# A gated cross-attention layer: the order of TensorE's work between attention groups, planned with a count of PSUM banks and copy times

## The chip, the cores and the metric

The kernel runs on one core of a Trainium2 chip. The metric is the device time of one execution in microseconds (us). Three runs of the kernel before took 2751.24, 2752.05 and 2752.25 us; the median is 2752.05 us. The profile is of one further execution, recorded by the hardware profiler.

## The reference, cut to what matters

Four batches of 256 rows of width 512 attend to a context of 1601 rows each, with 32 query heads in 8 key/value heads (4 query heads share one). Then a feed-forward part with a router follows. All is in float32.

```
x   (4, 256, 512)   ctx (4, 1601, 512)
q   = layernorm(x) @ Wq + bq                 # 8 heads x 4 groups x 128
k,v = split(ctx @ Wkv + bkv)                 # 8 heads x 128 each
a   = softmax(q k^T / sqrt(128))             # over the 1601 context rows
x   = x + tanh(g_xattn) * (a v @ Wo + bo)
x   = x + tanh(g_ffn) * ffn(layernorm(x))    # base product, router (2 of 8), low-rank parts
```

## The kernel before, in words

**Groups.** A head here is a key/value head with its four query heads. The 256 rows of a batch are cut in two (`l` is 0 or 1), so there are 4 x 8 x 2 = 64 groups, each with 128 rows times 4 query heads, which is 512 columns. In `run_group` (L866) TensorE alternates between score products of the current group (`score_unit`, matmul at L641) and value products of the group before it (`av_unit`, L691): 13 context tiles each, the last one with 65 rows. ScalarE copies each score tile out of PSUM (L648), VectorE keeps a running maximum (L593), then reduces it over partitions (`spread`, L595 to L615), subtracts it from the seven score tiles (L663), and ScalarE takes the exponential (L664). These steps are the softmax of the group; they go on while TensorE does something else.

**Windows.** That something else is done in the window behind each group, `window` (L890): q products for the next head (`q_steps`, four items `pq`, L354), the output product of the group before (`out_steps`, `po`, L714, added to x by VectorE at L721), and the products that make the keys and values of heads two at a time (`pair_steps`, L426). A pair's keys are made while the pair before it is being worked on; its values are made in the window behind its own first group. So the four groups of a pair have four windows, called W0 to W3 here:

- W0, even head, `l` = 0: the values of this pair, due at once
- W1, even head, `l` = 1: q of the odd head, due at once; the keys of the coming pair begin
- W2, odd head, `l` = 0: more of the keys; q of the next head begins
- W3, odd head, `l` = 1: the rest of both, due at once

At the end of a batch (heads 6 and 7) there are differences: the context and x of the next batch are transposed around the group and window of head 6, `l` = 1, and the next keys begin one window later.

**Block products.** Keys and values are made with seven block products in place of eight (a Strassen-like scheme), numbered 1 to 7 in `step` (L500). The context is halved, and each half is cut in two sub-blocks of 384 columns, so a pair has 14 product steps for keys and 14 for values, plus a `tail` for the last 65 context rows (L544). For each sub-block, products 1, 6, 5 and 3 add up in one PSUM bank called x, with a copy by ScalarE after each (L490, L494); product 2 has a bank z of its own, added by VectorE (L498); products 7 and 4 add up in a bank y, read by VectorE after 5 and after 4. So product 6 must wait for the copy after 1, and 4 for VectorE's add after 5, and so on.

**PSUM.** Five banks (`ps`, L109) serve all of this, two more hold scores, one holds the value product.

**Order.** TensorE's order is written out by hand (`manual_schedule`, L905): the order in which the Python functions are called is the order of its queue. The other engines' queues are ordered by the framework. A step is a tuple of cost, lag and function. `clock["now"]` counts planned nanoseconds: `mm_cost(512)` is 857. A `Task` holds steps in a fixed order, and is ready when its lag has passed (`ready`, L839). `window` sums one common credit over all tasks (cost divided by the windows left), takes the first ready task of the list at each step (`next_task`, L854), and afterwards `flush` (L859) does what is due. In a pair's task both sub-blocks alternate: 1 1 2 2 6 6 7 7 5 5 tail 3 3 4 4.

**Loads.** Weights of keys and values share one buffer (`load_pair`, L186), as do those of q (`load_wq`) and of the output (`load_wo`): each is loaded by SyncE's queue once the one before was used. GpSimd forms weight sums after the load (L209).

Of the kernel before, what the change touches and what calls it, by code (L numbers as in the profile page):

```python
# [15 lines left out]
P = 128  # L16
# [5 lines left out]
E = 8  # L22
# [5 lines left out]
def flamingo_kernel(  # L28
# [43 lines left out]

    nc = tc.nc
# [16 lines left out]
    NPAIR = len(pairs)  # L90
    AHEAD = 1
# [17 lines left out]
    ps = ctx.enter_context(tc.tile_pool(name="ps", bufs=5, space=bass.MemoryType.PSUM))  # L109
# [115 lines left out]
    def ffn_weight_steps():  # L225
# [21 lines left out]
        def step(o):  # L247
            def run():
                if o < NC:
                    load(o + 1)  # L250
                    dst, n = base_t[:, :, o * P : (o + 1) * P], P
                else:
                    dst, n = ra[:, :, E * R :], E
                transpose_rows(staged.pop(o), n, dst, f"base_{o}")
            return NC * TR_COST, LAG_DMA, run
# [8 lines left out]
    LAG_EVAC, LAG_COPY, LAG_O = 1500, 4000, 6000  # L264

    def x_steps(b, lag):
# [17 lines left out]
        def turn(l):  # L284
# [5 lines left out]
            return NC * TR_COST, lag, run  # L290
# [3 lines left out]
    def ctx_steps(b):  # L294
# [13 lines left out]
        def step(i):  # L308
            def run():
                if i + STAGE - 1 < KT:  # L310
                    load(i + STAGE - 1)
                turn_ctx(b, i, staged.pop(i))
            return NC * TR_COST, LAG_CTX, run
# [32 lines left out]
    def q_steps(b, h):  # L346
# [3 lines left out]
        def q_item(g):  # L350
# [13 lines left out]
            return NC * mm_cost(L), 0, run  # L364
# [12 lines left out]
    def plain_k_steps(b, h):  # L377

        def item(s, n):
# [13 lines left out]
            return NC * mm_cost(n), 0, run  # L393
# [3 lines left out]
    def plain_v_steps(b, hp):  # L397
# [3 lines left out]
        def item(i):  # L401
# [20 lines left out]
            return n * NC * mm_cost(WV), 0, run  # L422
# [3 lines left out]
    def pair_steps(kind, b, hp):  # L426
# [73 lines left out]
        def step(i, s):  # L500
# [26 lines left out]
            if is_k:  # L527
                return 2 * mm_cost(SUB), 0, run
            return SUB // P * 2 * mm_cost(HDIM), 0, run
# [177 lines left out]
    def out_steps(key):  # L707
# [20 lines left out]
        return [(G * mm_cost(D), LAG_O, project)] + (ffn_steps(b, l) if h == NKV - 1 else [])  # L728


    def ffn_steps(b, l):
# [78 lines left out]
        def final_item():  # L810
# [10 lines left out]
            (NC * TR_COST, LAG_NORM, turn_item),  # L821
            (NC * (mm_cost(E * R + E) + mm_cost(D) * (b == B - 1)), LAG_COPY, route_item),
            (TR_COST, LAG_ROUTE, mid_item),
            (mm_cost(D) * (1 if b == B - 1 else NC + 1), LAG_COPY, final_item),
# [7 lines left out]

    class Task:


        def __init__(self, steps, due=None):
            self.steps = deque(steps)
            self.due = due
            self.ready = clock["now"] + self.steps[0][1]  # L839
# [4 lines left out]
        def step(self):  # L844
            cost, _, fn = self.steps.popleft()
            fn()
            clock["now"] += cost
            if self.steps:
                self.ready = clock["now"] + self.steps[0][1]
            else:  # L850
                tasks.remove(self)
            return cost
# [37 lines left out]
    def window(now):  # L890

        credit = sum(t.cost() / (t.due - now + 1 if t.due is not None else 1) for t in tasks)
        while tasks and credit > 0:
            if (t := next_task()) is None:
                soon = min(t.ready for t in tasks)
                if soon > clock["now"] + LAG_EVAC:
                    break
                clock["now"] = soon
            elif t.steps[0][0] / 2 <= credit:
                credit -= t.step()  # L900
            else:
                break
        flush(lambda t: t.due is not None and t.due <= now)
# [148 lines left out]
```

## Time and profile before

| | |
|---|---|
| median of three runs | 2752.05 us |
| the profiled execution | 2752.54 us |
| its span, first to last instruction | 2750.8 us |
| mean granted clock of TensorE | 0.988 |
| TensorE matmul busy | 2653.8 us, 96% |
| VectorE busy | 2149.1 us, 78% |
| ScalarE busy | 1201.4 us, 44% |
| GpSimd busy | 166.4 us, 6% |
| DMA, mean rate | 38 GB/s |

In the profile PE is TensorE (PEld its weight loads), DVE is VectorE, ACT is ScalarE, POOL is GpSimd. A float32 matmul stands as two records, so a product over two chunks of 128 rows has four. A timeline line gives the start and length in us, the engine, the line in the kernel, the operation, and how many instructions were merged; what stands in square brackets is the idle time ahead of it and what ended it. A line of waits gives the total in us, the number of times and the longest. The two records overlap a little, so the time of a group is best read from its start to the start of the next one.

### The profile page before, as it was taken

The numbers are of one execution on the slowest core, as the hardware profiler recorded it, in microseconds if no ns is written. First come the engines' busy times: TensorE is split into PE (matmuls) and PEld (weight loads), VectorE is DVE, ScalarE is ACT, GpSimd is POOL, SyncE is SP. The second block draws the span as 40 slices with busy tenths as digits, with TensorE's granted clock in tenths as the row PEclk, the third lists the DMA queues.
The fourth block names the chain that finished last, engine by engine and source line by source line (L and its number), as shares of the span: only waits on it lengthen the run. The fifth ranks groups of instructions, "written<-read, shape, count | busy, mean of one in ns | idle before, by whom it ended". The sixth has DMA issues, their size and how long they took to land.

```text
span 2750.8 us, 25888 instructions
## 1 busy us (share of the span) xinstructions
PE 2653.8 (96%) x9317; PEld 1502.2 (55%) x9317; DVE 2149.1 (78%) x3309; ACT 1201.4 (44%) x1881; POOL 166.4 (6%) x141
## 2 busy tenths in 40 slices
PE   8999999999999999999999999999999999999997
PEld 6446555464654646546465464645556556464643
DVE  2877887878877778778886877887887777778877
ACT  2444443444534344445443444444444444434442
POOL 0001010100001000010010100100000010100100
PEclk9999999999999999999999999999999999999999
DMA  4101000121111001012010110100201101100100
GB/s 136 46 23 39 31 32 31 39 64 38 39 39 38 24 31 39 23 39 85 17 46 31 38 39 18 44 31 23 79 24 39 39 23 39 33 29 31 39 0 23
DMA packets 79289, 104.74 MB, mean 38 GB/s; under 512 B 4349, under 2 KB 37165, under 8 KB 79161
## 3 DMA queue, kind: packets, MB, share of 16 engines
q1 hardware_dynamic: 77720, 102.02, 11.7%
q8 instruction: 73, 1.20, 0.2%
q0 software_dynamic: 272, 0.53, 0.1%
q10 hardware_dynamic: 1168, 0.55, 0.1%
q14 instruction: 56, 0.45, 0.1%
HBM read 100.98 MB, written 2.10 MB: 37 GB/s over the span
## 4 chain that ended last, share of the span: by engine, by line
PE 81%; DVE 15%; ACT 2%; issue 1%; DMA 0%; ACTq 0%; DVEq 0%
PE sc L641 26%; PE av L691 22%; PE pq L354 7%; DVE p L663 5%; PE po L714 5%; PE pxv L466 5%; PE pxk L455 4%; PE pyv L466 2%; PE pyk L455 2%; DVE mx L593 1%; PE ptk L550 1%; PE pzv L466 1%; PE pzk L455 1%; PE py L761 1%; ACT p L664 1%
## 5 line engine op out<-in xcount | busy, mean ns | idle before, releaser
L641 PE MATMUL sc<-qT,kT 128*128 128x512 f32 (+1 forms) x1664 | 796.6, 604 | 32.1 <-ACT qT L361 19.5
L648 ACT COPY p<-sc 65x512 f32<-65x512 f32 x820 | 478.6, 585 | 757.0 <-PE sc L641 755.9
L691 PE MATMUL av<-p,v 65*128 65x512 f32 x1640 | 766.6, 593 | 1.6 <-ACT p L664 1.6
L593 DVE TENSOR_TENSOR mx<-mx,p 128x1024 f32<-128x1024 f32 x252 | 307.3, 1220 | 375.8 <-ACT p L648 374.0
L641 PEld LDWEIGHTS sc<-qT,kT 128*128 128x128 f32 (+1 forms) x1664 | 305.3, 189 | 440.2 <-issue 343.1
L691 PEld LDWEIGHTS av<-p,v 65*128 65x128 f32 x1640 | 310.1, 190 | 382.5 <-issue 379.8
L664 ACT ACTIVATE p<-p 65x512 f32<-65x512 f32 x442 | 425.6, 992 | 132.0 <-DVE p L663 123.9
L663 DVE TENSOR_TENSOR p<-p,res_mx 65x512 f32<-65x512 f32 x442 | 473.2, 1138 | 2.0
L593 DVE TENSOR_TENSOR sm<-sm,p 128x1024 f32<-128x1024 f32 x252 | 314.9, 1250 | 18.4
L714 PE MATMUL po<-wo,oT 128*128 128x512 f32 x512 | 232.0, 596 | 4.2 <-ACT oT L702 4.2
L354 PE MATMUL pq<-xnT,wq 128*128 128x256 f32 x1024 | 230.3, 379 | 0.0
L354 PEld LDWEIGHTS pq<-xnT,wq 128*128 128x128 f32 x1024 | 193.7, 190 | 41.8 <-issue 11.6
L209 POOL TENSOR_TENSOR wv<-wv 128x256 f32<-128x256 f32 x60 | 103.4, 1744 | 1612.0 <-DMA wv<-in_L_xattn_Wkv_dram 1610.8
L714 PEld LDWEIGHTS po<-wo,oT 128*128 128x128 f32 x512 | 96.7, 191 | 105.1 <-issue 93.6
L702 ACT ACTIVATE oT<-oT,biasT 128x512 f32<-128x512 f32 x64 | 46.2, 722 | 241.1 <-DVE oT L701 240.8
L588 DVE TENSOR_TENSOR mx<-p,p 128x1024 f32<-128x1024 f32 x63 | 79.0, 1254 | 92.1 <-ACT p L648 91.6
L209 POOL TENSOR_TENSOR wk<-wk 128x256 f32<-128x256 f32 x60 | 56.8, 967 | 789.0 <-DMA wk<-in_L_xattn_Wkv_dram 687.2
L490 ACT ACTIVATE kT<-pxk,biasT 128x384 f32<-128x384 f32 x120 | 68.4, 570 | 76.1 <-PE pxk L455 76.1
L455 PE MATMUL pxk<-ctxT,wk 128*128 128x384 f32 x240 | 100.0, 558 | 0.0
L494 ACT COPY v<-pxv 128x384 f32<-128x384 f32 x120 | 56.0, 472 | 85.6 <-PE pxv L466 85.3
L466 PEld LDWEIGHTS pxv<-wv,T 128*128 128x128 f32 x720 | 84.9, 192 | 7.2 <-issue 7.2
L466 PE MATMUL pxv<-wv,T 128*128 128x128 f32 x720 | 87.2, 275 | 0.0
(151 smaller groups left out, 2369.7 us busy)
## 6 DMA issues: line engine op xcount, KB each, us to landing
wq<-in_L_xattn_Wq_dram SPq DMA_DIRECT2D x32, 1024.0 KB, 5.2
wo<-in_L_xattn_Wo_dram SPq DMA_DIRECT2D x32, 1024.0 KB, 5.2
ctx<-in_ctx_dram SPq DMA_DIRECT2D x48, 256.0 KB, 2.7
wk<-in_L_xattn_Wkv_dram SPq DMA_DIRECT2D x60, 128.0 KB, 2.3
wv<-in_L_xattn_Wkv_dram SPq DMA_DIRECT2D x60, 128.0 KB, 2.3
xa<-in_x_dram SPq DMA_DIRECT2D x4, 512.0 KB
out_dram<-y SPq DMA_DIRECT2D x8, 256.0 KB, 2.0
base<-in_L_ffn_base_W_dram SPq DMA_DIRECT2D x4, 256.0 KB, 9.0
```

The costliest lines, as they stand in the source:

```text
L209: nc.gpsimd.tensor_tensor(w[:, out_], w[:, x_], w[:, y_], op)
L354: nc.tensor.matmul(pq[:, :L], w_t["q", b, h][:, c, g * HDIM : (g + 1) * HDIM], xnT_t[b][:, c, :], start=(c == 0), stop=(c == NC - 1),)
L455: nc.tensor.matmul(bk[:, :SUB], a(SLOT[i], c), operand(i, c, s, SUB), start=first and c == 0, stop=c == 1, skip_group_check=True,)
L466: nc.tensor.matmul(bk[:, t * HDIM : (t + 1) * HDIM], operand(i, c, s + t * P, P), a(SLOT[i], c), start=first and t == 0 and c == 0, stop=c ...
L588: nc.vector.tensor_tensor(acc, p[first], p[first + 1], op)
L593: nc.vector.tensor_tensor(acc, acc, p[j], op)
L641: nc.tensor.matmul(sc[:r, :], kT_t[b, h][:, i * P : i * P + r], qT_t[b, h][:, :, l * P : (l + 1) * P], start=True, stop=True,)
L648: nc.scalar.copy(p[:r, k, :], sc[:r, :])
L663: nc.vector.tensor_tensor(p, p, mb[:r].unsqueeze(1).to_broadcast([r, n, W]), ALU.subtract)
L664: nc.scalar.activation(p, p, AF.Exp, scale=scale)
L691: nc.tensor.matmul(av, v_t[b, h // 2][:r, i, h % 2, :], p_t[key][j][:r, k, :], start=(j == 0 and k == 0), stop=(j == NPAIR - 1 and k == le ...
L714: nc.tensor.matmul(po, oT_t[key][:, g, :], w_t["o", b, h][:, g, :], start=(g == 0), stop=(g == G - 1),)
```

## The change: what it does

Each step of a window now also says what it does with PSUM. `NBANK` is 5, and a list `free` holds the planned time at which each bank comes free. A step with a lag as its fourth member takes a bank for that long (2000 ns for ScalarE, 3000 for VectorE); product steps 1 and 7 take a bank without a term (`TAKE`), and 3 and 4 give it back. A task is ready when its lag has passed and a bank is free. Products 6, 5, 3 and 4 have lags of their own, for the copies that they follow.

The sub-blocks of a pair are no longer alternated in a fixed order. For values, each sub-block and the tail are tasks of their own, three in all, marked `chain`. For keys they are one task, one sub-block after the other, with the tail last. Within a sub-block the order is 1 2 6 7 5 3 4.

`window` gives each task a credit of its own: its cost over the windows left, or unlimited where it is due or has no due window. At each step it picks the task that can run first, a chain before others, then by place in the list. If the window's last step is not of a chain and a chain is ready, one more chain step is taken at the end.

Last, q of an odd head begins in W0 instead of W1 (except for the first head and across batches).

```diff
+    NBANK = 5
+    LAG_ACT, LAG_DVE = 2000, 3000
+    TAKE = -1
...
-            return NC * mm_cost(L), 0, run
+            return NC * mm_cost(L), 0, run, LAG_ACT
...
+            cost = 2 * mm_cost(SUB) if is_k else SUB // P * 2 * mm_cost(HDIM)
+            lag = {6: LAG_ACT - cost, 5: LAG_ACT - cost, 3: LAG_ACT, 4: LAG_DVE}.get(i, 0)
+            bank_use = {1: TAKE, 7: TAKE, 2: LAG_DVE, 3: (LAG_ACT,), 4: (LAG_DVE,)}.get(i)
+            return cost, lag, run, bank_use
...
-        subs = range(0, HK, SUB)
-        steps = [(0, 0, begin)]
-        for i in (1, 2, 6, 7, 5):
-            steps += [step(i, s) for s in subs]
-        if n:
-            steps.append((2 * NC * mm_cost(P), 0, tail))
-        for i in (3, 4):
-            steps += [step(i, s) for s in subs]
-        return steps
+        begin()
+        parts = [[step(i, s) for i in (1, 2, 6, 7, 5, 3, 4)] for s in range(0, HK, SUB)]
+        if n:
+            parts.append([(2 * NC * mm_cost(P), 0, tail, LAG_ACT)])
+        return parts
...
+    free = [0.0] * NBANK
     class Task:
+        @property
+        def ready(self):
+            use = self.use(self.steps[0])
+            if use is None or isinstance(use, tuple):
+                return self.since
+            return max(self.since, min(free, default=math.inf))
         def step(self):
+            step = self.steps.popleft()
+            step[2]()
+            clock["now"] += step[0]
+            self.credit -= step[0]
+            use = self.use(step)
+            if isinstance(use, tuple):
+                free.append(clock["now"] + use[0])
+            elif use is not None:
+                free.remove(min(free))
+                if use != TAKE:
+                    free.append(clock["now"] + use)
...
     def window(now):
-        credit = sum(t.cost() / (t.due - now + 1 if t.due is not None else 1) for t in tasks)
-        while tasks and credit > 0:
-            if (t := next_task()) is None:
-                soon = min(t.ready for t in tasks)
-                if soon > clock["now"] + LAG_EVAC:
-                    break
-                clock["now"] = soon
-            elif t.steps[0][0] / 2 <= credit:
-                credit -= t.step()
-            else:
-                break
-        flush(lambda t: t.due is not None and t.due <= now)
+        for t in tasks:
+            later = t.due - now if t.due is not None else 0
+            t.credit = t.cost() / (later + 1) if later > 0 else math.inf
+        step = None
+        while True:
+            can = [t for t in tasks if t.credit > 0 and t.steps[0][0] / 2 <= t.credit]
+            must = any(t.due is not None and t.due <= now for t in can)
+            if not can:
+                break
+            t = min(can, key=lambda t: (max(t.ready, clock["now"]), not t.chain, tasks.index(t)))
+            if t.ready > clock["now"] + LAG_EVAC and not must:
+                break
+            clock["now"] = max(clock["now"], t.ready)
+            t.step()
+            step = t
+        for t in tasks:
+            if step is not None and not step.chain and t.chain and t.ready <= clock["now"]:
+                t.step()
+                break
...
-                tasks.append(Task(pair_steps("v", *pair), now))
-            if nxt is not None and l == (0 if h % 2 == 1 and nxt[1] > 0 else NL - 1):
+                tasks.extend(Task(part, now, True) for part in pair_steps("v", *pair))
+            if nxt is not None and l == (0 if nxt[1] > 0 and hi > 0 else NL - 1):
                 tasks.append(Task(q_steps(*nxt), hi * NL + NL - 1))
...
-                tasks.append(Task(pair_steps("k", *coming), (hi | 1) * NL + NL - 1))
+                steps = sum(pair_steps("k", *coming), [])
+                tasks.append(Task(steps, (hi | 1) * NL + NL - 1, True))
```

The output product and the steps of the feed-forward part get a fourth member of the same kind (`LAG_DVE`, `LAG_COPY` or `LAG_ACT`), the transposes `LAG_EVAC`. No computation is added or removed.

More of the change, by code (lines that the diff above doesn't have):

```diff
@@ L108, in flamingo_kernel @@
     ps_av = ctx.enter_context(tc.tile_pool(name="ps_av", bufs=1, space=bass.MemoryType.PSUM))
-    ps = ctx.enter_context(tc.tile_pool(name="ps", bufs=5, space=bass.MemoryType.PSUM))
+    ps = ctx.enter_context(tc.tile_pool(name="ps", bufs=NBANK, space=bass.MemoryType.PSUM))
     def bank(name):
@@ L254, in run @@
                 transpose_rows(staged.pop(o), n, dst, f"base_{o}")
-            return NC * TR_COST, LAG_DMA, run
+            return NC * TR_COST, LAG_DMA, run, LAG_EVAC
         return [(0, 0, begin)] + [step(o) for o in range(NC + 1)]
@@ L289, in run @@
                 )
-            return NC * TR_COST, lag, run
+            return NC * TR_COST, lag, run, LAG_EVAC
         return [(0, 0, begin)] + [f(l) for l in range(NL) for f in (norm, turn)]
@@ L312, in run @@
                 turn_ctx(b, i, staged.pop(i))
-            return NC * TR_COST, LAG_CTX, run
+            return NC * TR_COST, LAG_CTX, run, LAG_EVAC
         return [(0, 0, begin)] + [step(i) for i in range(KT)] + [(0, 0, lambda: ctx_sums(b))]
@@ L392, in run @@
                 )
-            return NC * mm_cost(n), 0, run
+            return NC * mm_cost(n), 0, run, LAG_ACT
         return [item(s, n) for s, n in chunks]
@@ L421, in run @@
                 )
-            return n * NC * mm_cost(WV), 0, run
+            return n * NC * mm_cost(WV), 0, run, LAG_ACT
         return [item(i) for i in range(0, KT, 2)]
@@ L526, in run @@
                     add_to(1, 0, s, bk)
-            if is_k:
-                return 2 * mm_cost(SUB), 0, run
-            return SUB // P * 2 * mm_cost(HDIM), 0, run
+            cost = 2 * mm_cost(SUB) if is_k else SUB // P * 2 * mm_cost(HDIM)
+            lag = {6: LAG_ACT - cost, 5: LAG_ACT - cost, 3: LAG_ACT, 4: LAG_DVE}.get(i, 0)
+            bank_use = {1: TAKE, 7: TAKE, 2: LAG_DVE, 3: (LAG_ACT,), 4: (LAG_DVE,)}.get(i)
+            return cost, lag, run, bank_use
         n = LK - TAIL
@@ L726, in project @@
                 load_wo(*heads[n])
-        return [(G * mm_cost(D), LAG_O, project)] + (ffn_steps(b, l) if h == NKV - 1 else [])
+        return [(G * mm_cost(D), LAG_O, project, LAG_DVE)] + (ffn_steps(b, l) if h == NKV - 1 else [])
     def ffn_steps(b, l):
@@ L820, in ffn_steps @@
             (0, 0, norm_item),
[L821 to L824, printed above, removed]
+            (NC * TR_COST, LAG_NORM, turn_item, LAG_COPY),
+            (NC * (mm_cost(E * R + E) + mm_cost(D) * (b == B - 1)), LAG_COPY, route_item, LAG_DVE),
+            (TR_COST, LAG_ROUTE, mid_item, LAG_ACT),
+            (mm_cost(D) * (1 if b == B - 1 else NC + 1), LAG_COPY, final_item, LAG_DVE),
         ]
@@ L831, in flamingo_kernel, with __init__, use @@
     tasks = []
+    free = [0.0] * NBANK
     class Task:
-        def __init__(self, steps, due=None):
+        def __init__(self, steps, due=None, chain=False):
             self.steps = deque(steps)
             self.due = due
-            self.ready = clock["now"] + self.steps[0][1]
+            self.chain = chain
+            self.since = clock["now"] + self.steps[0][1]
+            self.credit = 0.0
+        @staticmethod
+        def use(step):
+            return step[3] if len(step) > 3 else None
+        @property
[4 more added lines that the diff above has]
+            return max(self.since, min(free, default=math.inf))
         def cost(self):
@@ L844, in step @@
         def step(self):
-            cost, _, fn = self.steps.popleft()
-            fn()
-            clock["now"] += cost
+            step = self.steps.popleft()
[9 more added lines that the diff above has]
+                    free.append(clock["now"] + use)
             if self.steps:
-                self.ready = clock["now"] + self.steps[0][1]
+                self.since = clock["now"] + self.steps[0][1]
             else:
                 tasks.remove(self)
-            return cost
+            return step[0]
     def next_task(most=math.inf):
```

## The prediction, made before the kernel was run

> **What bounds the kernel now.** I read the page's busy shares first, then the list of TensorE's waits, then the timelines of a pair's four windows, then the granted clock.
>
> ```profile
> span 2750.8 us, 25888 instructions
> PE 2653.8 (96%) x9317; PEld 1502.2 (55%) x9317; DVE 2149.1 (78%) x3309; ACT 1201.4 (44%) x1881; POOL 166.4 (6%) x141
> ...
> PE ptk L550 <- DVE xa L721: 32.0, 12, 2.7
> PE sc L641 <- ACT qT L361: 19.5, 19, 3.5
> ...
> PE ptk L550 <- ACT kT L552: 6.1, 15, 0.4
> ```
>
> TensorE is the bound, and its idle time is all that an order can win. Two waits matter: the tail of the keys for an addition to x (12 times), and scores for a q copy (19 times: 16 of 0.56 us, 3 of 3.5 us). TensorE's and then VectorE's timeline of one W2:
>
> ```profile
> 1000.73 2.74 PE L455 MATMUL pxk<-T,wk 128*128 128x384 f32 x8
> 1003.31 3.60 PE L714 MATMUL po<-wo,oT 128*128 128x512 f32 x8
> 1009.57 1.11 PE L550 MATMUL ptk<-ctxT,wk 128*128 128x65 f32 x8 [2.66 <-DVE xa L721]
> 1011.08 0.66 PE L550 MATMUL ptk<-ctxT,wk 128*128 128x65 f32 x4 [0.41 <-ACT kT L552]
> 1011.58 0.61 PE L550 MATMUL ptk<-T,wk 128*128 128x65 f32 x4
> 1012.02 2.79 PE L455 MATMUL pxk<-ctxT,wk 128*128 128x384 f32 x4
> 1014.60 3.28 PE L641 MATMUL sc<-qT,kT 128*65 128x512 f32 x6
> ...
> 1000.42 7.50 DVE L663 TENSOR_TENSOR p<-p,res_mx 65x512 f32<-65x512 f32 x7
> 1007.84 1.01 DVE L498 TENSOR_TENSOR kT<-pyk,kT 128x384 f32<-128x384 f32 x2
> 1008.77 0.74 DVE L721 SCALAR_TENSOR_TENSOR xa<-po,gates,xa 128x512 f32<-128x512 f32 x1
> ```
>
> The tail needs a bank; x and y of both sub-blocks and `po` hold all five. `po`'s is freed by L721, which stands in VectorE's queue behind seven softmax subtractions. In each of the four windows these end 11.07 us after the window's start (884.73 after 873.66, 922.12 after 911.05, 968.74 after 957.67, 1007.92 after 996.86). Then the clock drops:
>
> ```profile
> 1012.00:1015.40 3.40, 3.40 (x7) 1.52 (x7) 3.09 (x4) 0.87 (x2) 0.00 (x0) 0.52 0.00 0
> ```
>
> This row of stretches has the granted clock third from its end: 0.52. Four records take 2.58 us (1012.02 to 1014.60) for 1.29, six score records 3.11 for the 2.65 that they take after W0 and W1: 1.75 us lost. A W2 thus loses 2.67 + 0.41 + 1.75 = 4.83 us.
>
> **What the Trainium skill says.** "TensorE: Matmul & The Clock Gate", Part 1: the array runs at half clock after an idle window of about 3.4 us and returns after a busy one. The trace agrees on the length (3.41 us each) but here an idle of 2.67 us was enough, 12 of 12 times; 1.41 us (at 764) was not. "PSUM — Partial Sum Buffer", section Engine vs sequencer instructions: ScalarE's and VectorE's queues are strict FIFO. The trace agrees: additions ready early stand behind the seven subtractions. The same page, Specifications: eight banks per partition; that is the five, two and one of this kernel.
>
> **The change, part by part.** Costs on TensorE, start to start: a k product 1.29 us (2.58 for 8 records), a v product 1.34 (2.68 for 24), a q item 1.73 (6.91 for four), `po` 3.43, the k tail 1.75 without its wait. Work is only moved between windows, so what counts is idle time. I followed the new rule by hand, with the code's own costs and lags, to get each order, and laid the trace's copy times over it (primes: second sub-block; times from the window's start).
>
> *W2:* credit is half the keys left, 6.67 us, enough for five steps, half of q is two items. At 0 the chain's 3 is ready and runs to 1.29; 4 is ready 3.0 later, at 4.29, so both q items come first, to 4.73; 4 runs to 6.02; 1 and 2, being of the chain, come before `po` (ready at 6.0) and end at 8.60; 6 is not ready until 9.31, so `po` is next and 6 last. Order: 3 q q 4 1 2 po 6, 13.3 us. The tail is gone. Banks: y (until VectorE's add), x', z' and `po` are four, the q copies are short. No wait is left: 12 x 4.83 = 58 us won. What covers the late VectorE adds is that nobody in W2 wants their banks; were it gone, the wait of 2.67 would be back.
>
> *W3:* 7' q 5' q po 3' 4' tail'. Step 4' accumulates in y, so it waits for VectorE's add after 5'. TensorE is at 10.75 us (1.29 + 1.73 + 1.29 + 1.73 + 3.43 + 1.29); the subtractions end at 11.07, the add takes 0.54, a semaphore 0.05: 11.66, a wait of 0.9. The tail's second half waits 0.41 for ScalarE as it did in W2. The 0.56 for q goes, since q is no longer last. Net +0.75 x 12 = +9. Queued behind 4' are the tail and the next scores.
>
> *W0:* 1 2 1' 6 7 2' 5 6' 7' 3 5' tail 4 3' po 4' q q. Step 7' wants a sixth bank at 8 x 1.34 = 10.72 us; x, z, x', y, z' are out, and z comes free with VectorE's add, at 11.66 if that stands behind the subtractions. Wait 0.95 x 15 = +14. Bounds: 0, because an add that is ready early can slip in ahead of the subtractions, as this one 3.5 us into its window does:
>
> ```profile
> 694.18 0.52 DVE L498 TENSOR_TENSOR kT<-pyk,kT 128x384 f32<-128x384 f32 x1
> 694.62 7.48 DVE L663 TENSOR_TENSOR p<-p,res_mx 65x512 f32<-65x512 f32 x7
> ```
>
> and 2.7, W2's old wait, if another VectorE job or two go first. I take 0.95, the order seen in three of the four windows above, where the adds follow the subtractions. `po`'s weight load for the next head leaves later, 23.5 us into W0, and lands 5.2 us later; it is used some 33 us after that.
>
> *W1:* 1 2 q 6 7 po 5 q. Now q is last and the scores wait 0.56 for its copy: +0.56 x 12 = +7. The rule for one extra chain step misses: step 3 is ready at 13.59, the plan's clock stands at 13.31.
>
> *Batch ends* (3): the window behind head 6's second group ends with q; its copy is late behind the exponentials (3.50 us, then half clock: six score records in 4.17, so 1.5). Now half of q is in W0 and the rest first: up to 5 x 3 = 15 won. But VectorE is full there (from 610.96 to 651.37 it idles 2.1 us), so a window shortened by q hands part of it to later waits: I take 9.
>
> *Loads:* the keys' weights are used to the end of W3 (some 15 us) instead of 4 us into it, and SyncE's queue has the values' loads and then q's behind that. Landing 2.3, four GpSimd sums of 1.74: done about 10 us into a group of 22.6. Hidden; a lateness past 12 us would show as a wait of W0. K sums (four of 0.97) have W0's end to W1. The longer hold on x and y costs nothing else.
>
> *VectorE in shorter windows:* W1 and W2 shrink to 13.3 us, so a group repeats after 13.3 + 22.6 = 35.9. VectorE was busy 33.1 of the 37.4 us from 871.04 to 908.43 (idle 2.11 and 2.21). 2.8 us are spare, so subtractions still start on time, and value products need their first exponential some 11 us after it is made.
>
> Sum: 2750.8 - 58 + 9 + 14 + 7 - 9 = 2713.8 of span. The profiled execution took 2752.54, 1.7 more than its span, and the median is 2752.05. Less 37 that is 2715.
>
> **Rivals.**
>
> *Clock gate in the new waits (slower).* W3 and W0 trade one long wait for short ones on the same VectorE queue, behind the same subtractions. If these grow enough to gate the clock, each costs 1.75 more: 27 x 1.75 = 47, so 2715 + 47 = 2762. If a wait grows to W2's old 2.67 besides, 27 x 1.75 again: 2810. It decides at 37 / 27 = 1.4 us more per window. For: VectorE has only 2.8 us spare, and W3's two waits add up to 1.3 us within a few us. Against: 1.41 did not gate.
>
> *Half of it lost.* Only W3 gates: 12 x 1.75 = 21, so 2736.
>
> *No difference.* W3 gates and waits 1.3 more: 37 gained, 37 lost, 2752. This is also the case that the model's order is not what binds, since the new banks are waited for on the same engine.
>
> *More won.* The adds of z slip in ahead of the subtractions (14 less) and the batch ends give all 15 (6 less): 2695. For: 694.18. Against: in the window at 873.66 the add of a product that ended at 876.2 stood behind subtractions that began at 877.23.
>
> **How the numbers follow.** Likeliest, 2715: 0.45, with its own range of 2700 to 2730 (waits of W0 at zero, or W3's 1.3 us longer). More won, 0.16; half lost, 0.09; no difference, 0.08; slower, 0.22, since the framework orders the other engines' queues anew when TensorE's changes, and I can follow only TensorE's. Faster by over 0.2% (5.5 us, about what a measurement of this kernel can tell from no change) is 0.45 + 0.16 + 0.09 = 0.70, within it 0.08, slower 0.22. Below 2692 I leave 0.06, a third of the case of more; above 2765 some 0.13, the worse half of the slower one: range 2692 to 2765.
>
> **What would show it.** Right: no wait of `ptk` for L721 and about twelve fewer stretches of half clock; new waits of about 0.9 us of `pyk` for L498 in W3 and of a `pyv` in W0; q waits of 0.56 after W1 and not after W3; three long q waits gone. Wrong: a wait of a product for L498 of over 2 us, followed by half clock; value products waiting for L664 (VectorE late through short windows); sums at L209 or weights ending a TensorE wait; more half-clock stretches than the 17 or so lost before.

## The result, and the profile after

The changed kernel takes 2764.03 us (median of 6, 2762.8 to 2765.68), the kernel before 2752.15 us (median of 6 with these): a ratio of 1.0039, interval 1.0026 to 1.0052. It is slower by 0.4%. The forecast of 2715 us, faster, has the wrong sign; 2764 lies inside the range, where the slower rival stood, but not by that rival's mechanism; that the number agrees with it is luck.

First the head of the page after:

```profile
span 2762.1 us, 25736 instructions
...
PE 2655.4 (96%) x9317; PEld 1505.9 (55%) x9317; DVE 2131.4 (77%) x3309; ACT 1200.7 (43%) x1881; POOL 113.0 (4%) x141
```

TensorE's busy time is nearly the same (2653.8 us before), so most of the 11.3 us by which the span has grown is idle time. TensorE's waits after (total, times, longest, in us):

```profile
PE sc L645 <- ACT p L652: 25.1, 12, 3.8
PE pxv L472 <- ACT v L500: 13.9, 3, 4.6
PE ptk L558 <- ACT kT L560: 12.6, 15, 2.0
PE pyk L461 <- DVE kT L504: 9.5, 11, 1.4
PE pyv L472 <- DVE v L504: 8.6, 12, 0.7
PE sc L645 <- ACT qT L367: 6.9, 10, 1.8
PE pxk L461 <- ACT kT L496: 5.4, 3, 1.8
```

The wait of `ptk` for the addition to x, 32.0 us before, is gone. So are the three q waits of 3.5 us, but three waits of 3.85 us, of scores for a score copy, have come in their place (see below). The two waits foreseen for VectorE are there (`pyk`, `pyv`). Four lines were not foreseen, and all four name ScalarE: scores for a score copy (25.1, before 8.0), a value product for a copy three times for 4.6 us, a wait of up to 2.0 us for the tail's copy, and a key product for a copy three times for 1.8 us.

Adding up the trace from window start to window start shows where the 11.3 us of span come from:

| stretch | before | after | difference |
|---|---|---|---|
| start to W0 of the second pair | 235.4 | 231.6 | -3.8 |
| two pairs inside a batch, four times | 4 x 327.6 | 4 x 321.55 | -24.2 |
| three batch ends (W0 of a batch's last pair to W0 of the next batch's second) | 1044.4 | 1079.9 | +35.5 |
| W0 of the last pair to the end | 160.6 | 164.4 | +3.8 |

Inside a batch the forecast holds almost exactly. TensorE's timeline of one W2 and then of the W3 behind it, after (start, length, instruction; idle time in brackets):

```profile
998.88 1.45 PE L461 MATMUL pxk<-ctxT,wk 128*128 128x384 f32 x4
1000.17 3.62 PE L360 MATMUL pq<-xnT,wq 128*128 128x256 f32 x16
1003.62 1.45 PE L461 MATMUL pyk<-T,wk 128*128 128x384 f32 x4
1004.91 1.45 PE L461 MATMUL pxk<-ctxT,wk 128*128 128x384 f32 x4
1006.20 1.45 PE L461 MATMUL pzk<-ctxT,wk 128*128 128x384 f32 x4
1007.49 3.60 PE L718 MATMUL po<-wo,oT 128*128 128x512 f32 x8
1010.92 1.45 PE L461 MATMUL pxk<-T,wk 128*128 128x384 f32 x4
1012.21 1.02 PE L645 MATMUL sc<-qT,kT 128*65 128x512 f32 x2
...
1046.21 1.56 PE L461 MATMUL pyk<-T,wk 128*128 128x384 f32 x4 [0.68 <-DVE kT L504]
...
1049.01 0.66 PE L558 MATMUL ptk<-ctxT,wk 128*128 128x65 f32 x4 [0.41 <-ACT kT L560]
```

W2 is 13.33 us long (forecast 13.3), in the order worked out by hand, 3 q q 4 1 2 po 6, without a wait or a half clock. Step 4' of W3 starts 11.60 us after its window's start at 1034.61 (forecast 11.66).

At a batch's end it is another matter. TensorE's timeline of the first window of the second batch:

```profile
736.54 1.50 PE L472 MATMUL pzv<-wv,ctxT 128*128 128x128 f32 x12
742.67 5.15 PE L472 MATMUL pxv<-wv,T 128*128 128x128 f32 x24 [4.63 <-ACT v L500]
```

And ScalarE's in the same stretch:

```profile
734.18 1.28 ACT L668 ACT_TABLE_LOAD   x1 [1.81 <-DVE p L667]
735.47 5.46 ACT L668 ACTIVATE p<-p 65x512 f32<-65x512 f32 x6
740.83 0.46 ACT L500 COPY v<-pxv 128x384 f32<-128x384 f32 x1
741.19 1.06 ACT L668 ACTIVATE p<-p 128x1024 f32<-128x1024 f32 x1
742.15 0.47 ACT L500 COPY v<-pxv 128x384 f32<-128x384 f32 x1
```

Products 1' and 6 end by about 735.2. Their copies stand in ScalarE's queue behind a table load and six exponentials, and start only at 740.83 and 742.15; product 5 needs the second of them. TensorE idles 4.63 us, then runs at half clock for two stretches on end. In the regular W0 the queue is mixed differently. ScalarE at 911.6, where no table has to be loaded:

```profile
915.94 0.63 ACT L668 ACTIVATE p<-p 65x512 f32<-65x512 f32 x1 [1.83 <-DVE p L667]
916.48 0.46 ACT L500 COPY v<-pxv 128x384 f32<-128x384 f32 x1
917.08 1.06 ACT L668 ACTIVATE p<-p 128x1024 f32<-128x1024 f32 x1
```

Where does the table load come from? The layer norms' square root (L170) and the exponential need different tables, so each square root is followed by a load back. The loads back by the line that has to make them (count, then busy us in all and mean ns, then idle time ahead of them), before:

```profile
L778 ACT ACT_TABLE_LOAD x7 | 9.0, 1283 | 0.1
L664 ACT ACT_TABLE_LOAD x4 | 5.1, 1283 | 8.1 <-DVE p L663 8.1
```

And all of them after:

```profile
L170 ACT ACT_TABLE_LOAD x11 | 14.1, 1283 | 0.2
L668 ACT ACT_TABLE_LOAD x10 | 12.8, 1283 | 14.9 <-DVE p L667 14.9
L782 ACT ACT_TABLE_LOAD x1 | 1.3, 1283 | 0.0
```

The 11 loads for the square root are the same in both, and so are the 11 back. Before, seven of the eleven loads back fall on the router's small exponential (L778), where ScalarE waits for VectorE anyway (after the load at 737.00 it still waits 0.75 us for the first subtraction). After, the router's product `pm` stands behind the values, because these are marked `chain` and the router is not; ten of the eleven now fall on the softmax (L668), between subtractions and copies, where four did before. The Trainium skill ("ScalarE: Activation LUTs", What ACT_TABLE_LOAD costs) gives 1283 ns for a load, as the trace has it; the further 1380 ns of draining that it adds do not show here (the load at 734.18 ends at 735.46, the first exponential starts at 735.47). The price here is not the 1.28 us but where they fall: the run with the router first, below, has as many loads and wins 16.5 us.

The window behind head 6's second group has shrunk from 15.62 to 8.50 us, since half of q went to W0 (3.50 of the 15.62 us were the old wait for q's copy). TensorE's records behind it:

```profile
617.27 1.88 PE L645 MATMUL sc<-qT,kT 128*65 128x512 f32 x4
623.00 1.12 PE L645 MATMUL sc<-qT,kT 128*128 128x512 f32 x2 [3.85 <-ACT p L652]
```

And ScalarE's:

```profile
615.73 1.28 ACT L668 ACT_TABLE_LOAD   x1 [1.12 <-DVE p L667]
617.02 5.46 ACT L668 ACTIVATE p<-p 65x512 f32<-65x512 f32 x6
622.38 0.56 ACT L652 COPY p<-sc 65x512 f32<-65x512 f32 x1
```

The next group begins while ScalarE is still at the exponentials of the last. It waits 3.85 us for a score copy, runs at half clock and takes 29.07 us instead of 23.92. Of the 7.12 us by which the window shrank, 3.50 are the old wait and 3.46 the work that W0 had taken over; the group gives back 5.15. So the wait has only moved, from q's copy to a score copy behind the same exponentials. VectorE has next to no time to spare here. The only idle times that its timeline marks from the window's start at 608.77 to the group's end at 646.34 are these two:

```profile
631.26 1.23 DVE L592 TENSOR_TENSOR mx<-p,p 128x1024 f32<-128x1024 f32 x1 [0.67 <-ACT p L652]
...
640.29 1.23 DVE L597 TENSOR_TENSOR mx<-mx,p 128x1024 f32<-128x1024 f32 x1 [0.19 <-ACT p L652]
```

It is busy for 36.1 of these 37.57 us. The group behind the next window is longer than before too, by 2.1 us at the first batch end and 3.8 at the two others (24.48 and 26.19 us against 22.39): scores wait 1.9 us for a score copy there, and at the second and third end half clock follows.

A third loss is in W3 of a batch's first pair, where only the last steps 3' and 4' are left and the tail comes early, among the exponentials:

```profile
883.06 0.66 PE L558 MATMUL ptk<-ctxT,wk 128*128 128x65 f32 x4 [2.04 <-ACT kT L560]
...
884.11 5.23 PE L718 MATMUL po<-wo,oT 128*128 128x512 f32 x8
```

The output product takes 5.23 us there in place of 3.6. The granted clock after three of these waits is third from the end of each row (stretch, its length, busy time and instructions of five engines, clock, DMA share, GB/s):

```profile
624.36:627.77 3.41, 3.41 (x6) 1.31 (x5) 3.41 (x6) 0.50 (x2) 0.00 (x0) 0.51 0.00 0
740.41:747.23 6.82, 4.56 (x21) 4.56 (x22) 6.72 (x9) 2.69 (x5) 0.00 (x0) 0.51 0.00 1
883.77:887.18 3.41, 3.41 (x8) 1.80 (x8) 3.38 (x5) 2.39 (x4) 0.00 (x0) 0.51 0.43 118
```

### The profile page after: what moved, and what is told of

Read it like the earlier page. It is cut to its first block, busy times and chain, and to the rows that moved or that the text cites. A ratio compares the mean times of both kernels' runs of the same rounds, so it can differ in the third digit from the quotient of the medians.

```text
span 2762.1 us, 25736 instructions
## 1 busy us (share of the span) xinstructions
PE 2655.4 (96%) x9317; PEld 1505.9 (55%) x9317; DVE 2131.4 (77%) x3309; ACT 1200.7 (43%) x1881; POOL 113.0 (4%) x141
## 4 chain that ended last, share of the span: by engine, by line
PE 76%; DVE 17%; ACT 5%; issue 2%; DMA 0%; ACTq 0%; DVEq 0%
PE sc L645 25%; PE av L695 21%; DVE p L667 7%; PE po L718 5%; PE pq L360 5%; PE pxv L472 4%; PE pxk L461 3%; ACT p L668 3%; PE pyv L472 2%; PE pyk L461 2%; DVE mx L597 2%; PE py L765 1%; PE pzk L461 1%; PE ptv L558 1%; PE ptk L558 1%
## 5 line engine op out<-in xcount | busy, mean ns | idle before, releaser
L645 PE MATMUL sc<-qT,kT 128*128 128x512 f32 (+1 forms) x1664 | 796.0, 604 | 36.6 <-ACT p L652 25.1
L668 ACT ACTIVATE p<-p 65x512 f32<-65x512 f32 x442 | 425.4, 991 | 100.8 <-DVE p L667 94.8
L718 PE MATMUL po<-wo,oT 128*128 128x512 f32 x512 | 238.8, 611 | 2.6 <-ACT oT L706 2.6
L367 ACT ACTIVATE qT<-pq,biasT 128x256 f32<-128x256 f32 x128 | 60.1, 469 | 167.9 <-PE pq L360 167.6
L212 POOL TENSOR_TENSOR wv<-wv 128x256 f32<-128x256 f32 x60 | 59.6, 1013 | 1712.6 <-DMA wv<-in_L_xattn_Wkv_dram 1711.4
L472 PE MATMUL pxv<-wv,T 128*128 128x128 f32 x720 | 95.4, 290 | 13.9 <-ACT v L500 13.9
L472 PEld LDWEIGHTS pxv<-wv,T 128*128 128x128 f32 x720 | 91.1, 205 | 14.5 <-ACT v L500 14.5
L461 PE MATMUL pxk<-T,wk 128*128 128x384 f32 x240 | 87.8, 488 | 5.4 <-ACT kT L496 5.4
L472 PEld LDWEIGHTS pxv<-wv,ctxT 128*128 128x128 f32 x720 | 86.4, 192 | 7.2 <-issue 7.2
```

The costliest lines, as they stand in the source:

```text
L367: nc.scalar.activation(qT_t[b, h][:, g, :], pq[:, :L], AF.Identity, bias=bias_of("q", h * G + g))
L461: nc.tensor.matmul(bk[:, :SUB], a(SLOT[i], c), operand(i, c, s, SUB), start=first and c == 0, stop=c == 1, skip_group_check=True,)
L472: nc.tensor.matmul(bk[:, t * HDIM : (t + 1) * HDIM], operand(i, c, s + t * P, P), a(SLOT[i], c), start=first and t == 0 and c == 0, stop=c ...
L645: nc.tensor.matmul(sc[:r, :], kT_t[b, h][:, i * P : i * P + r], qT_t[b, h][:, :, l * P : (l + 1) * P], start=True, stop=True,)
L668: nc.scalar.activation(p, p, AF.Exp, scale=scale)
L718: nc.tensor.matmul(po, oT_t[key][:, g, :], w_t["o", b, h][:, g, :], start=(g == 0), stop=(g == G - 1),)
```

## The experiments

Theory A throughout: the new order is right inside the batches and loses at their ends, where what TensorE next needs stands behind exponentials in ScalarE's queue. The rivals differ from run to run. Times are medians; ratios are to the kernel before, with intervals.

**Old order at the batch ends (e1_old_ends).** A flag brings the old `window`, the old alternating steps and the old start of q back for seven windows around each batch end, and q of head 7 waits until its own window in the last batch too.

```diff
+            mode["old"] = (h == NKV - 2 and l == 1) or h == NKV - 1 or (b > 0 and h < 2)
...
     def window(now):
+        if mode["old"]:
+            return window_old(now)
```

> The changed kernel, but the seven windows around the end of each batch (from head 6, second group, to the next batch's head 1, second group), and head 7's q in the last batch, keep the order and the rule of before. Theory A (the new order wins in the windows inside a batch and loses around the batch ends): each batch end takes 348 us again instead of 358.4, 360.6 and 360.9, which is 35.5 less, and the last end 3.8 less, so 2764 - 39 = 2725, some 27 under the kernel before. Rival B (the windows inside a batch only look shorter, and what they lose in VectorE's spare time is paid back at the ends, whatever the order there): the ends stay above 355 each and the time at 2750 or more.

Measured: 2730.44 us, ratio 0.9915 (0.99 to 0.9929); A said 2725. The two pairs inside a batch keep 321.55 us, and the first batch end takes 348.6 against 358.4. The change was worth making, inside the batches.

**A bank of its own for the tail's second half (e2_tail_two_banks).**

```diff
             for f in range(2):
+                if is_k and f == 1:
+                    bk = bank(f"pu{nm}")
```

> The changed kernel, but the second half of the keys' tail has a PSUM bank of its own, so that it needn't wait for ScalarE's copy of the first half. Theory A (each of the 15 waits of ptk for ScalarE, 12.6 us in all, and the four stretches of half clock behind the 2.04 us ones come from the one bank): 12.6 and about 4 x 1.7 less, so 2764 - 19 = 2745. Rival B (ScalarE's queue holds up what comes next just as long, since the next scores or the q copies stand behind the same exponentials): no more than 5 us less, 2759 or above.

Measured: 2743.18 us, 0.9967 (0.9954 to 0.998); A said 2745. W3 of the second batch's first pair goes from 15.20 to 11.25 us and the `ptk` wait is not there; two pairs inside a batch go from 321.55 to 320.32. So it was the copy of the other half of the same bank, 0.41 us eleven times, and about 2.0 us with its half clock in the first pair of each of the four batches. The Trainium skill ("PSUM — Partial Sum Buffer", PSUM bank collisions) says that TensorE must not write a bank while another engine reads it in the same 32 partitions, whichever columns; the framework's wait and this run agree with it.

**No square root (e3_no_root).**

```diff
-        tc.keep_in_program_order(nc.scalar.activation(sd, sd, AF.Sqrt))
+        tc.keep_in_program_order(nc.scalar.activation(sd, sd, AF.Identity))
```

> The changed kernel, but the layer norms leave out the square root: ScalarE runs Identity in its place, an instruction of the same size and place, so that no table for the root and none for the exponential behind it has to be loaded (22 loads of 1.28 us go). What is computed is then a norm by the variance. Theory A (at a batch end a table load ahead of the exponentials makes them late, and ScalarE then takes six in a row while copies that products wait for stand behind them): the wait of 4.6 us of product 6 in the first window of batches 1 to 3 falls under 1 us and its two windows of half clock go (3 x 7), the 1.8 us wait two windows later goes (3 x 2), the scores behind head 6 wait 1.3 less each (3 x 1.3): about 30 less, 2734. Rival B (the batch ends are long because VectorE is full there, as the prediction had it; the root's work on VectorE is unchanged): less than 6 us less, 2758 or above.

Measured: 2737.39 us, 0.9944 (0.9929 to 0.9959); A said 2734. The first window of the second batch goes from 35.43 to 29.29 us. ScalarE there, of this kernel:

```profile
732.44 0.63 ACT L668 ACTIVATE p<-p 65x512 f32<-65x512 f32 x1 [1.83 <-DVE p L667]
732.97 0.46 ACT L500 COPY v<-pxv 128x384 f32<-128x384 f32 x1
733.58 1.06 ACT L668 ACTIVATE p<-p 128x1024 f32<-128x1024 f32 x1
```

Without the table load the copies stand between the exponentials again, as in the regular W0. One part of the expectation failed: the group behind the shrunken window did not get shorter (29.23 us against 29.07). Its first wait fell from 3.85 to 1.57, but others of 0.39, 0.30 and 1.89 us followed. VectorE is busy for 36.1 of the 37.73 us of window and group. That loss is not the table's.

**q of head 7 late, as before (e4_q7_late).**

```diff
-            if nxt is not None and l == (0 if nxt[1] > 0 and hi > 0 else NL - 1):
+            if nxt is not None and l == (0 if nxt[1] > 0 and hi > 0 and h != NKV - 2 else NL - 1):
```

> The changed kernel, but all four q products of head 7 are made in the window behind head 6's second group, as before the change, instead of two there and two in the window ahead of it. Theory A (that window got too short, 8.5 us, so that the next scores meet ScalarE still at its exponentials): the group behind it takes about 24 us again instead of 29, but q is last in the window and its copy waits behind the same exponentials (3.5 us as before the change), so of 6.7 us lost per end some 1 to 3 come back, and 3.8 at the last end: 2764 - 10 = 2754. Rival B (the length of that window is of no matter, VectorE sets the end of the group): unchanged within 3 us, 2761 or above.

Measured: 2753.34 us, 1.0001 (0.9992 to 1.0009); A said 2754. The window is back at 15.62 us, with its old q wait of 3.50, and the group behind it at 24.02. So it was the short window that made that group long, and the early half of q, which I had booked as a gain, cost 10.7 us over the run (2764.03 - 2753.34), about 3 of them at the last end. That the group ends earlier with a longer window does not say which engine set its end: VectorE and ScalarE both had more time.

**The same edit in the kernel before (e6_before_no_root).** A control for the table loads.

```diff
-        tc.keep_in_program_order(nc.scalar.activation(sd, sd, AF.Sqrt))
+        tc.keep_in_program_order(nc.scalar.activation(sd, sd, AF.Identity))
```

> The kernel before, with the square root of the layer norms replaced by an identity on ScalarE (the layer norms then divide by the variance, so that the output is another one), so that the tables of ScalarE are loaded once. Theory A (the order of before keeps ScalarE's late copies off TensorE's path except for the q behind head 6, so it has little to win here): some 3 x 3 us less, about 2743, while the changed kernel won 26.6 us by the same edit. Rival B (table loads cost the order of before as much as the new one): 2727 or less.

Measured: 2752.83 us, 1.0002 (0.9994 to 1.0011). Neither number was met; the rival is refuted, and of A's 9 us nothing shows. The q wait behind head 6 falls from 3.5 to 2.0, the rest stays. The same edit that wins 26.6 us in the changed kernel wins nothing in the kernel before: the table loads cost only in combination with the new order.

**Values of a batch's first pair alternating (e5_v0_alternate).** These values are one task in the old order, not marked as a chain.

```diff
+                if h == 0:
+                    a, c, tl = pair_steps("v", *pair)
+                    order = [f for k in range(5) for f in (a[k], c[k])] + tl
+                    order += [a[5], c[5], a[6], c[6]]
+                    tasks.append(Task([f[:1] + (0,) + f[2:3] for f in order], now))
+                else:
```

> The changed kernel, but the values of the first pair of batches 1 to 3 are made in the order of the kernel before: the two sub-blocks alternate, 1 1' 2 2', the output product, 6 6' 7 7' 5 5' tail 3 3' 4 4'. The table load and the six exponentials ahead of ScalarE's copies stay. Theory A (product 6' meets a copy held up behind the table load and the exponentials; with 2, 2' and the output product in between it comes too late to meet it): the wait of 4.63 us falls under 1 us and the half clock after it goes, some 7 us less in each of three windows: 2764 - 21 = 2743. Rival B (the table load is the whole cause, whatever the order): 2760 or more.

Measured: 2737.32 us, 0.9943 (0.9928 to 0.9958). The 4.63 us wait is gone (window 29.79 us), but the expectation was wrong in a premise: with the values no longer a chain, the router's product went ahead of them as well, and seven loads fell on the router again. So this run changes the order of the values and the place of the load at once, and the next two take them apart. (It also names the product wrongly: by the order of the copies it is 5 that waits for the copy of 6.)

**Router first, values in the new order (e9_router_first).**

```diff
-            t = min(can, key=lambda t: (max(t.ready, clock["now"]), not t.chain, tasks.index(t)))
+            head0 = now % (NKV * NL) == 0
+            t = min(can, key=lambda t: (max(t.ready, clock["now"]),
+                                        not (t.chain or head0 and t.steps[0][2].__name__ == "route_item"),
+                                        tasks.index(t)))
```

> The changed kernel, but the router product pm of the first rows of a batch is put ahead of the values in the first window of a batch, where the kernel before has it; the values keep the new order. The router's own exponential then loads the table while ScalarE still waits for VectorE's subtractions. Theory A (what holds up the copy is a table load that falls between the subtractions and the copies): the wait of 4.63 us and its half clock go, some 6 us in each of three windows, and a little in the window after: 2764 - 20 = 2744. Rival B (the new order asks for its copies too early, wherever the table is loaded): 2758 or more.

Measured: 2747.5 us, 0.9976 (0.9967 to 0.9984), 16.5 less than the changed kernel (A said 20). ScalarE in the first window of the second batch, of this kernel:

```profile
735.64 1.28 ACT L782 ACT_TABLE_LOAD   x1
...
738.09 0.63 ACT L668 ACTIVATE p<-p 65x512 f32<-65x512 f32 x1 [0.76 <-DVE p L667]
738.62 0.46 ACT L500 COPY v<-pxv 128x384 f32<-128x384 f32 x1
```

The load is made in the time in which ScalarE waits for VectorE, and the window takes 29.31 us with a wait of 0.65. The loss of the window after, where the router of the other rows is still late (1.93 us), stays.

**Values alternating, router late (e10_alternate_router_late).** As e5, with the router held back until at most four of the values' steps are left.

```diff
+            if now % (NKV * NL) == 0 and any(len(t.steps) > 4 and t.due == now for t in tasks):
+                can = [t for t in can if t.steps[0][2].__name__ != "route_item"]
```

> The kernel with the values of a batch's first pair in the alternating order, but with the router product only after most of the values, so that the table load stands behind the subtractions, as in the changed kernel. Theory A (the alternating order asks for a copy only two products and an output product later, so it does not meet the late one): as with the router product first, 2737 to 2744. Rival B (the alternating order was saved by the early table load alone): a wait of over 2 us in the first window of a batch, 2752 or more.

Measured: 2739.26 us, 0.9951 (0.9936 to 0.9967). ScalarE in the first window of the second batch:

```profile
733.01 0.48 ACT L500 COPY v<-pxv 128x384 f32<-128x384 f32 x1 [0.35 <-PE pxv L472]
734.47 1.28 ACT L668 ACT_TABLE_LOAD   x1 [0.98 <-DVE p L667]
```

The load is back in front of six exponentials, but the copies of 1 and 1' were made before it (the second is the one at 733.01), and no value product waits. Product 5, which needs the copy of 6 (741.13), comes only at 744.58. So either repair is enough: the wait of 4.63 us needs the late load and the new order together, and neither alone.

**Old ends and the tail in two banks (e7_old_ends_two_banks).** e1, with the second bank of e2 in the windows of the new order.

```diff
+        chained = not mode["old"]
...
+                if is_k and f == 1 and chained:
+                    bk = bank(f"pu{nm}")
```

> The kernel with the new order inside the batches and the old one around the batch ends, and besides a bank of its own for the second half of the keys' tail in the windows of the new order. Theory A (what the tail waits for is the copy of its other half in the same bank, and the time stays won): nine waits of 0.41 and one of 2.0 with its half clock of 1.7 go, 2730.4 - 3.7 - 3.7 = 2723. Rival B (the wait moves to the q or the scores behind it): 2729 or more.

Measured: 2719.51 us, 0.9879 (0.9862 to 0.9895). `ptk` waits for its copy 6 times instead of 15 (2.4 us instead of 7.7 in all). A said 2723. Against e1 this is 10.9 us less; e2 had won 9.2 where e7 has the second bank too (4.9 inside the batches, 4.3 ahead of the second pair). The two gains add up.

**Less of the old order, and two waits more taken away (e8_all).** e7, and besides:

```diff
-            mode["old"] = (h == NKV - 2 and l == 1) or h == NKV - 1 or (b > 0 and h < 2)
+            mode["old"] = (h == NKV - 2 and l == 1) or h == NKV - 1 or (b > 0 and h == 0 and l == 0)
...
-            if step is not None and not step.chain and t.chain and t.ready <= clock["now"]:
+            if step is not None and not step.chain and t.chain and t.ready <= clock["now"] + 500:
...
+                    steps = parts[0] + parts[1][:-1] + parts[2] + parts[1][-1:]
```

> As the one with old ends and the tail in two banks, and besides: the old order only from the second window of head 6 to the first window of the next batch, so that the second to fourth windows of a batch's first pair have the new order too; the tail ahead of the last step 4 of the keys; and a chain step more at the end of a window where it is ready within 500 ns. Theory A (each of these takes a wait of TensorE away and nothing replaces it): nine waits of 0.9 in the fourth window, nine of 0.56 behind the second, and three to four us in each of three first pairs, so about 2722 - 8 - 5 - 4 = 2705. Rival B (the windows get shorter and the time comes back as waits for ScalarE or VectorE): 2720 or more.

Measured: 2689.55 us, 0.977 (0.9755 to 0.9784), better than A. Two pairs inside a batch take 316.96 us, 3.35 less than in e7: 13.4 in all, as expected. The three batch ends take 17.7 us less. The expectation named three to four us in each of three first pairs but put only 4 into its sum; measured are 6 in each: W1 is 1.3 us longer than in e7, W2 3.3 and W3 3.7 shorter. W3 of this kernel on TensorE:

```profile
1012.98 0.61 PE L561 MATMUL puk<-ctxT,wk 128*128 128x65 f32 x4
...
1017.38 1.45 PE L462 MATMUL pyk<-T,wk 128*128 128x384 f32 x4
```

`puk` is the tail's second half in its own bank. No wait is left in the window: the further chain steps at the ends of W1 and W2 put 5' into W2 already, so that VectorE's add after it is long done when 4' wants the bank. The three edits were not run apart.

**The output product last behind head 6 (e11_all_q_first).** e8, with the output product taken from the list in that one window and run at its end.

```diff
         if mode["old"]:
-            return window_old(now)
+            out = tasks.pop(0) if now % (NKV * NL) == (NKV - 2) * NL + 1 and now < (B - 1) * NKV * NL else None
+            window_old(now)
+            if out is not None:
+                tasks.insert(0, out)
+                out.step()
+            return
```

> The fastest kernel so far (2689.6) with one more edit: in the window behind head 6's second group the output product is last, behind all of q. Theory A (a wait there is for whatever stands behind the table load and the six exponentials in ScalarE's queue; with q's copies made before these and the output product as cover, the scores meet the exponentials some 1 to 1.5 us before their end and without the clock being halved): the q wait of 3.5 us becomes 1 to 1.5 us for a score copy, with the half clock of 1.5 gone: 3 x 3.5 = 10 less, 2679. Rival B (the scores wait for their own copies as long as they did for q's): 2688 to 2692.

Measured: 2682.18 us, 0.9744 (0.973 to 0.9759), the fastest of all, 70.8 us under the kernel before (2752.94 beside it); A said 2679. The 3.5 us wait is 1.51, three times, and no half clock follows (in e8 it followed two of the three). In one point A was wrong: it is still a q copy that is waited for, since two of them stand between the exponentials:

```profile
606.52 2.52 ACT L678 ACTIVATE p<-p 65x512 f32<-65x512 f32 x3
608.95 0.45 ACT L367 ACTIVATE qT<-pq,biasT 128x256 f32<-128x256 f32 x1
609.30 1.04 ACT L678 ACTIVATE p<-p 128x1024 f32<-128x1024 f32 x1
610.25 0.46 ACT L367 ACTIVATE qT<-pq,biasT 128x256 f32<-128x256 f32 x1
```

## Why the prediction was wrong, step by step

- **W2, -58: right.** The order, the length of 13.3 us and the end of the wait and of its half clock are as forecast, in regular pairs. In a batch's first pair (of batches 1 to 3) the window takes 18.92 us after and 17.79 before, with feed-forward products (`py`) that moved into it.
- **W3, +9, and W0, +14: right in the regular pairs.** Step 4' starts 11.60 us into W3 and 7' 11.60 us into W0 (1083.96 after 1072.36); I had 11.66 for both. The add stands behind the subtractions, as I chose, and did not slip in. The waits are a little shorter than forecast, 0.68 and 0.72 us for 0.9 and 0.95, since TensorE gets there 0.2 us later. For the first pairs of the batches the forecast had the same; there W0 and W3 went otherwise (see the batch ends).
- **W1, +7: right in kind.** q's copy is waited for 0.56 us, but in 8 windows and not in 12: in the first pair of a batch a step of the keys comes last, and not q.
- **A regular pair**: -4.83 + 0.75 + 0.95 + 0.56 = -2.6 forecast, 163.80 to 160.78 = -3.0 measured; the shorter waits are the difference.
- **Batch ends, "up to 5 x 3 = 15 won ... I take 9": the step that failed.** By the forecast's own terms the stretches around the three ends should have won 14 us (9, and 2.6 for each of three first pairs, less 0.95 for W0 of each last pair); they lost 35.5. The last end should have lost 0.95 and lost 3.8. That is a miss of some 52 us, against about 4 more won elsewhere than forecast, which makes the 48 us between the spans of 2713.8 and 2762.1. Three things were wrong in it.
  - First, the 15 us were not there to be won. "VectorE is full there" was right, and weighed more than I gave it: VectorE's work in the second window of head 6 and the group behind it is 36.8 us of 39.54 before and 36.1 of 37.57 after, so the two could become some 3 us shorter at most, and W0 had to take 3.46 us of q for that. They became 1.97 us shorter, and the group behind the next window grew by 2.1 to 3.8. In e11 all of q stands in this window again, and window and group take only 36.77 us, with VectorE busy for 36.1 of them. That VectorE's work sets this length, and ScalarE's queue only which product waits, is read from these traces; no run made that work less. Taking the early q back won 10.7 us (e4).
  - Second, I let the order of W0 worked out for a regular pair stand for a batch's first pair too, although the router's product moves there from the first place behind the values, with the table load that its exponential makes: I had counted moved products but not what they trigger on ScalarE (e9: 16.5 us).
  - Third, I took the tail's wait for 0.41 us everywhere; where W3 has little left, the tail meets the exponentials and waits 2.04 us, and the clock is halved (e2: 20.9 us, the 0.41s included).
- **The rival "clock gate in the new waits" (2762)** has the right time and the wrong cause: the waits for VectorE in W3 and W0 stayed at 0.7 us in regular windows and halved no clock. "The framework orders the other engines' queues anew" stood in the forecast as a reason for doubt without a price; that is what happened at ScalarE, with the copies of the values and the scores.
- **Loads and GpSimd's sums: hidden, right.** No wait of TensorE in the list ends at a weight load's sum.

The gains of e2, e4 and e9 against the changed kernel are 20.9, 10.7 and 16.5 us, 48.1 together. Of e2's gain 4.9 us lie inside the batches and 4.3 ahead of the second pair; the other 38.9 are about the 39.3 lost at the ends against the kernel before. So the three causes are of the size of that loss. No run takes all three away at once, though, a half-clock stretch more or less changes such a sum by 1.7 us (half of 3.41), and of the 14 us that the ends should have won besides, 9 were not there to be won (the first point); the other 5 stay open.

## What to carry to other kernels

When an order of TensorE's work is made with a model of copy times, look at each place where the copying engine does something else in the loop's body: a constant lag of 2 us held inside the batches and was over 5 us short where a table load stood before six exponentials. When a step is moved, ask what its consumers do on the other engines, small ones too: here a 136-column product carried a table load with it. And a window made shorter is a gain only if the engine that must be through by its end can be: compare its busy time in window and group with the length that you hope for (here 36.1 us of VectorE's work).

## What the runs showed of the hardware

- Whether an idle time halves TensorE's clock depends on when it falls. The same q wait of 3.49 to 3.50 us was followed by no half clock at 612.47 in e8 and at 1290.38 in e1 (six score records in 2.87 us), by half clock for the time of about one stretch at 620.23 in e1 (the same six in 4.17), and for over 5 us at 1270.75 in e8 (5.38). In the changed kernel the half-clock stretches shown above begin 116.05 and 143.36 us apart, 34 and 42 times 3.413 us. The Trainium skill ("TensorE: Matmul & The Clock Gate", Part 1) says of the activity window that it is 3413 ns long and free-running; these runs agree. It speaks of a whole idle window; here less was enough, at some places in the window. The tail's wait of 2.04 us stands 25 times in the profiles of all runs, and 21 times half clock follows (in the changed kernel four times in four). Counted in steps of 3.413 us from a half-clock stretch of the same execution, the four exceptions begin 2.0 to 2.6 us into a step (the waits that end at 204.07 in e1, 202.82 in e3, 875.17 and 1546.96 in e10; the output product behind them takes 3.65 us, not 5.23), and the 21 others outside of that.
- So the time after such a wait is partly chance. e1's profiled execution took 2724.55 us and its three others 2730 to 2731; that this is the gate's phase is argued, not shown.
- With a table load of 1.28 us behind VectorE's first subtraction, six exponentials stand ahead of the copy in ScalarE's queue (735.47); without a load (e3, 732.44), or with the load earlier (e9, 738.09), one does. The load alone doesn't make the row of six: in e5 six in a row follow no load (736.38, and no product waits), and in e11 only three follow one (606.52). Where exactly the framework draws that line wasn't tried.
